# The first 40 microseconds of a fused graph-attention and gated-graph kernel: another route for adj's left halves, for the attention row and for the small weights, and other ranks

## The chip, the cores and the metric

The kernel runs on one core of one Trainium2 chip. The metric is the device time of one execution in microseconds. Three executions of the kernel before took 1454.94, 1455.84 and 1456.82 us; the median, 1455.84 us, is what the changed kernel is compared with. The profile is of one further execution.

A core has five engines, each with its own instruction stream executed in order: PE (TensorE, matrix products), DVE (VectorE), ACT (ScalarE), POOL (GpSimd) and SP (SyncE, here only an issuer of transfers). PE's loading of the stationary operand is listed as PEld. Transfers are issued on queues of SP, ACT and POOL and are carried by 16 DMA engines. Engines wait for each other by semaphores.

## The reference

There are 16 items x[b] of 1024 x 128, and one 0/1 matrix adj of 1024 x 1024, the same for all of them. Layer 0 is a graph attention:

```python
h = x @ others_weight
u1 = h @ a1;  u2 = h @ a2            # att_weight, two halves of 128
e = u1[:, idx1] + u2[:, idx2]        # pairs of neighbouring nodes
e = jnp.where(e >= 0, e, ALPHA * e)
att = jax.nn.softmax(jnp.where(adj > 0, e, NEG_BIG), axis=1)
x = layernorm(x + einsum('bik,bkl->bil', att, h) + x @ self_weight)
```

Layer 1 is five steps of a gated graph network, with h = x to begin with, and a second residual and normalisation at the end:

```python
m = adj @ h
u3 = h @ u3_w.T + u3_b
z = sigmoid([m, m] @ w3_w.T + w3_b + u3)
r = sigmoid([m, m] @ w4_w.T + w4_b + u3)
hv = tanh([m, m] @ w5_w.T + w5_b + (r * h @ u5_w.T + u5_b))
h = (1 - z) * h + z * hv
# after five steps: x = layernorm(x + h)
```

## The kernel before, in words

**Layout.** Of a matrix with 1024 rows, `NC` = 8 blocks of 128 rows lie on the 128 partitions; [...]nearly every matrix product is issued in halves of 512 columns. `adj` stays in SBUF for the whole run, in the type float32r; being 0 and 1 it is exact there. A product of a float32 matrix h with adj is made as two float32r products: `split` writes h's high part on ACT (`blk_h`, L636) and the remainder on DVE (L640), and `product` (L648) multiplies both with the same block of adj. Both parts together are the reference's float32 product. Other matrices (gates, h = x @ W) are multiplied in float32, which in the profile appear as two records for one instruction.

**Attention without a 1024 x 1024 softmax.** As e of one row depends on pairs of nodes, exponentials are taken once per column and not per entry. `wv_` (L414 to L423, DVE) forms the products of `others_w` with the two halves of the attention row; `spread_` (L767, PE) makes the scores of all nodes from item 0 on all partitions (`ps_p`); `lrelu_`, `exps_`, `exp_` and `larger_` (L770 to L783) turn them into `pb`, the exponentials. `z_` (L855, DVE, eight instructions of 128 x 512) multiplies each left half of adj with them and sums the rows. `rz_` (L874 to L878) takes the reciprocals, in two groups of four blocks for item 0. `hi_` and `lo_` (L907 ACT, L913 DVE) scale h by these into `blk`, and `po_` (L648 on `ps_acc_po`) multiplies `blk` with adj. The residual and self term is `px` (L970, L984), made with `wsi` = self_weight + identity. For items 4 to 7 that term is made ahead of time (L472, `ps_ahead`) and stored (PX). Item 1's exponentials are spread by L799. All other items have theirs fetched from DRAM.

**Gated steps.** Items go in pairs. For every pair and step, `ps_acc` collects adj times both items' h; `m`, `ps_g_r`, `gz` and `ps_g_v` are the gates' inputs, made with u3 (L1234), wm (L1244, L1260) and u5h (L1261). `wm`, `u5h` and the biases are prepared by `sums` after `own_weights`: one transposition on PE (L410, `ps_g_b`) turns the five bias rows into columns.

**Order.** Nothing is scheduled by the compiler. Every operation is put into a `Plan` with an engine, an estimated length, a rank, and the names it reads and writes. `Plan.order()` walks a model of time: whenever an engine is free it takes, of the operations whose inputs are there, the one with the lowest rank. The instructions are then issued in this order, and the hardware's engines follow it in order. Ranks come from the table `D` (one number per kind of operation) and from `NUDGE` (one number per item or per item and step). `dve`, `act`, `pe` and `sp` are one-line calls of `plan.add`; `lands` tells the plan when a transfer is thought to have landed.

**The start.** `early_loads` issues the first transfers on SP's and ACT's queues: x of item 0 in two halves, `others_w`, the attention row broadcast from DRAM to 128 partitions (128 KB, L351), adj as eight pieces of two row blocks by one half (512 KB each) into float32 tiles `staged[k][e]` (the trace calls them `blk_boot`), self_weight, x of item 1. `adj_tables(c)` casts these into `adj` (L494 for the left half, four on DVE and four on ACT; L497 for the right half, on ACT, which counts its row's ones as well). `late_loads` then sends ten small weights and biases (L381 to L388) from POOL's queue, after a copy that waits for the last piece of adj. `constants` writes the identity and some constants with POOL. Two fill matmuls (L440) and `IDLE` = 60 pairs of transposes of the identity (L436, rank 9000: taken when nothing else is ready in the plan) occupy PE; nobody reads their results. [...]

Of the kernel before, what the change touches and what calls it, by code (L numbers as in the profile page):

```python
# [10 lines left out]
F32 = mybir.dt.float32  # L11
F32R = mybir.dt.float32r
I32 = mybir.dt.int32
AF = mybir.ActivationFunctionType
# [3 lines left out]
P = 128  # L18
N = 1024
HALF = 512  # L20
NC = N // P
# [4 lines left out]
SHIFT = 40.0  # L26
# [6 lines left out]
AHEAD = range(4, 8)  # L33
LATE = 3001
TURNED = {(0, 0), (0, 1), (7, 2), (7, 3)}
IDLE = 60
NUDGE = {(3, 2): -0.6, (3, 3): 0.3, (0, 1): -0.5, (1, 1): 0.45, (2, 3): -0.2, (3, 1): -1.2, (3, 0): 0.6, (0, 2): 0.25, (2, 2): -0.6, (1, 4): -1.2, (1, 3): 0.3, (0, 3): -0.6, (1, 2): -0.15, (4, 0): -0.1, (2, 0): 1.2, (2, 1): 0.05, (4, 4): -0.3, (2, 4): -0.15, (7, 3): -0.75, (5, 4): 1.2, (4, 3): 1.25, (6, 3): -1.5, (6, 4): -0.6, (8, 2): 0.15, 10: 0.05, (11, 3): -1.2, (11, 4): 0.3, (7, 2): 0.3, (8, 3): -0.6, (12, 3): -0.45, (13, 3): -0.9, (12, 0): 1.15, (10, 3): -0.35, (8, 4): 0.05, (12, 4): -0.3, (12, 1): -0.05, (11, 2): -0.15, 12: -0.05, (13, 4): 1.2, (13, 0): 1.2, (11, 1): 0.05, (12, 2): 0.15, (10, 4): 0.1, (15, 0): -0.6, (14, 2): -0.6}


class Plan:  # L40
# [103 lines left out]
def kernel(  # L144
# [79 lines left out]
    def exact(pools):  # L224
# [48 lines left out]
        def T(t, dtype=None, shape=None):  # L273
            if t not in tiles:
                _, sh, dt, _ = kinds[t[0]]
                tiles[t] = places[t[0]].tile(
                    shape or sh, dtype or dt, tag=t[0], name="_".join(map(str, t)).replace("-", "n")
                )
            return tiles[t]
# [16 lines left out]
        def pe(*a, **k):  # L296
            plan.add("PE", *a, **k)

        def dve(*a, **k):
            plan.add("DVE", *a, **k)  # L300

        def act(*a, **k):
            plan.add("ACT", *a, **k)

        def sp(*a, **k):
            plan.add("SP", *a, **k)


        D = dict(m=-0.05, pu=1.4, u=0.95, pr=0.55, pz=0.85, r=0.25, pv=1.05, z=1.3, hv=-0.7, h=1.2, tr=2.55, o=6.35, ln=2.5, out=4.4, l1=-9, l2=-4, l3=-2, l4=-5.5, l5=-7.25)
        D.update(l6=-1.35, l7=-1, l8=-2, q=10, s=4.2, even=1, base=-1, q1=-6, b1=4, lz=-4, l1_0=-9, l2_0=-4, lz_0=-4, l3_0=-2, l4_0=-4, l5_0=-7, l6_0=-1.5, l7_0=-1, l8_0=-2)  # L310
        D.update(l1_1=-10, l2_1=-9, lz_1=-4, l3_1=-2, l4_1=-4, l5_1=-7, l6_1=-1.5, l7_1=-1, l8_1=-2, tab=8, tabc=1, cl=-5.9, ca=-50, cr=-51, px=-3.5, own=-2, ownw=-4.6)

        def on_pe(b, what):

# [20 lines left out]
        def W(name):  # L335
            return T(boot)[:, cols[name]]

        ws = ("T", "ws")
        staged = [[("blk", "boot", k, e) for e in range(2)] for k in range(NC // 2)]
        x0 = ("xt", 0)  # L340

        def adj_half(k, e):
            hs = slice(e * HALF, (e + 1) * HALF)
            rows = adj_t[2 * k * P : 2 * (k + 1) * P, hs].rearrange("(c p) n -> p c n", p=P)
            return T(staged[k][e], F32, [P, 2, HALF]), rows

        def early_loads():
            nc.sync.dma_start(T(x0)[:, HALF:N], x_t[0][:, HALF:N])
            nc.scalar.dma_start(T(x0)[:, 0:HALF], x_t[0][:, 0:HALF])
            nc.sync.dma_start(wo[:, 0:P], others_w)  # L350
            nc.scalar.dma_start(T(ws)[:, P : 3 * P], att_w.rearrange("k o -> o k").to_broadcast([P, 2 * P]))  # L351
            nc.sync.dma_start(*adj_half(0, 0))
            nc.scalar.dma_start(*adj_half(1, 0))
            nc.sync.dma_start(*adj_half(0, 1))
            nc.scalar.dma_start(*adj_half(1, 1))
            nc.sync.dma_start(W("ws"), self_w)
            for k in range(2, NC // 2):
                for e in range(2):
                    nc.sync.dma_start(*adj_half(k, e))
            nc.sync.dma_start(T(("xt", 1)), x_t[1])  # L360

        sp(
            9500,
            -103,
            early_loads,
            writes=[(boot, "early"), (ws, "early"), (x0, "early"), (("xt", 1), "early"), *((t, "early") for k in staged for t in k)],
        )

        def lands(ns, what):
            plan.add("DMA", ns, -103, lambda: None, writes=what, lag=0)  # L370

        lands(4700, [(x0, 0), (x0, 1)])
        lands(400, [(("wo",), 0), (ws, "att")])
        for ns, k, e in ((3600, 0, 0), (1400, 1, 0), (1000, 0, 1), (1400, 1, 1), (1600, 2, 0), (1400, 2, 1), (1400, 3, 0), (1400, 3, 1)):
            lands(ns, [(staged[k][e], 0), *([(boot, "ws")] if (k, e) == (2, 0) else [])])
        lands(1400, [(("xt", 1), 0), (("xt", 1), 1)])

        def late_loads():
            nc.gpsimd.tensor_copy(mark, T(staged[3][1])[0:1, 0, 0:1])
            for j, w in enumerate((w3_t, w4_t, w5_t)):  # L380
                nc.gpsimd.dma_start(  # L381
                    W("w345")[:, 256 * j : 256 * (j + 1)].rearrange("p (t e) -> p t e", t=2),
                    w.rearrange("(t p) e -> p t e", p=P),
                )
            nc.gpsimd.dma_start(u3, u3_t)
            nc.gpsimd.dma_start(u5, u5_t)
            for j, v in enumerate((w3_b, w4_b, w5_b, u3_b, u5_b)):
                nc.gpsimd.dma_start(T(ws)[j : j + 1, 3 * P : 4 * P], v.rearrange("(o p) -> o p", o=1))  # L388

        plan.add(  # L390
            "POOL",
            11000,
            -80,
            late_loads,
            reads=[(staged[3][1], 0)],
            writes=[(boot, "late"), (("uw",), 0), (ws, "b")],
            lag=2500,
        )

        def constants():  # L400
            make_identity(nc, ident)
            nc.gpsimd.memset(shift, -SHIFT)
            nc.gpsimd.memset(ones, 1.0)
            nc.gpsimd.memset(mhalf, -0.5)

        plan.add("POOL", 1400, -100, constants, writes=[(("ident",), 0), (("ones",), 0)])


        def column_(t, cols, n):
            nc.tensor.transpose(T(t)[:, 0:n], T(ws)[0:n, cols], ident[0:n, 0:n])  # L410

        def wv_():
            for two in range(2):
                nc.vector.scalar_tensor_tensor(  # L414
                    T(("look", "wv"))[:, two * P : (two + 1) * P],
                    wo[:, 0:P],
                    1.0,
                    T(ws)[:, (1 + two) * P : (2 + two) * P],
                    ALU.mult,
                    ALU.mult,  # L420
                    accum_out=wv[:, two : two + 1],
                )
            nc.vector.tensor_tensor(  # L423
                T(ws)[:, 0:P], wv[:, 0:1].to_broadcast([P, P]), wv[:, 1:2].to_broadcast([P, P]), ALU.add
            )
# [2 lines left out]
            nc.vector.tensor_copy(wo[:, P : P + 2], wv)  # L428
            nc.vector.tensor_copy(wo[:, P + 2 : P + 3], T(ws)[:, 0:1])

        dve(650, -101, wv_, reads=[(ws, "att"), (("wo",), 0)], writes=[(ws, 0), (("look", "wv"), 0)])
        dve(190, -65, wo_, reads=[(ws, 0)], writes=[(("wo",), 1)])

        def idle_():
# [55 lines left out]
        def adj_tables(c):  # L490
            st = staged[c // 2]

            def left(copy):
                copy(adj[:, c, 0:HALF], T(st[0])[:, c % 2])  # L494

            def right():
                nc.scalar.activation(adj[:, c, HALF:N], T(st[1])[:, c % 2], AF.Identity, accum_out=cnt[:, c : c + 1])  # L497

            if c < 4:
                dve(420, D["cl"], lambda: left(nc.vector.tensor_copy), reads=[(st[0], 0)], writes=[(("A",), c, 0)])  # L500
            else:
                act(A, D["ca"], lambda: left(nc.scalar.copy), reads=[(st[0], 0)], writes=[(("A",), c, 0)])
            act(640, D["cr"], right, reads=[(st[1], 0)], writes=[(("A",), c, 1)])

        def quarter(i, j):
            return lambda c: adj[:, 4 * i + c, j * HALF : (j + 1) * HALF]
# [149 lines left out]
        def layer0(b):  # L658
# [190 lines left out]
            rank = rank0(b) + lv("lz")  # L849
            for c in range(NC):  # L850

                st = staged[c // 2][0]

                def z_(c=c, st=st):
                    nc.vector.scalar_tensor_tensor(  # L855
                        T(junk),
                        T(st)[:, c % 2] if b == 0 else adj[:, c, 0:HALF].bitcast(F32),
                        1.0,
                        pairs()[:, c // 4, :],
                        ALU.mult,  # L860
                        ALU.mult,
                        accum_out=T(zs)[:, c : c + 1],
                    )

                entries = (st, 0) if b == 0 else (("A",), c, 0)
                dve(740, rank, z_, reads=[(pb, 0), (pb, 1), entries], writes=[(zs, c), (junk, 0)])


# [874 lines left out]
```

## Time and profile before

| what | us |
| --- | --- |
| median of three executions | 1455.84 |
| the profiled execution | 1455.08 |
| its span, first to last instruction | 1453.5 |
| PE busy | 1435.8 (99%) |
| DVE busy | 1159.7 (80%) |
| ACT busy | 897.4 (62%) |
| POOL busy | 193.5 (13%) |
| mean granted clock of PE | 0.997 |

Some landmarks of the first 60 us, from the order of time in the trace:

| event | us from the span's start |
| --- | --- |
| x of item 0 landed | 4.64 |
| attention row landed on all partitions | 7.06 |
| first piece of adj landed, last piece | 9.75, 18.11 |
| function table loaded on ACT | 10.89 to 12.17 |
| first and last row sum z of item 0 | 14.43, 22.37 |
| ten small loads issued by POOL | 18.30 to 25.89 |
| first product `ps_acc_po` of item 0 | 30.23 |
| transposition of the biases | 40.93 |
| first product `ps_acc` of the gated steps | 47.38 |

How to read it: a line of the order of time has the start, the duration (from the first start to the last end where several instructions stand in one line), the engine, the line of the kernel, the operation and "result <- inputs". A bracket at its end tells how long the engine was idle before it and what ended that. In tables by stage, each engine has its busy time in the stretch and the number of its instructions; then come PE's granted clock, the share of DMA engines busy, and the GB/s moved. An engine is busy also with work that nobody uses, such as the idle transposes.

### The profile page before, as it was taken

How to read it: one execution, taken by the hardware profiler on the slowest of the kernel's cores; microseconds unless marked ns; L12 is line 12 of the kernel's file. 1: busy time of each engine (PE TensorE's matmuls, PEld its weight loads, DVE VectorE, ACT ScalarE, POOL GpSimd, SP SyncE). 2: the span in 40 equal slices, each digit the busy share in tenths (PEclk: the TensorE clock that was granted, in tenths of full speed). 3: DMA queues.
4: the chain of work that ended last, by engine and by line, in shares of the span. 5: the costliest groups of instructions: out<-in, count | busy, mean ns of one | idle time of the engine just before them, and what ended most of it. 6: DMA issues, size and time to landing. Idle time of an engine off the chain costs nothing. (4 is left out here: it accounts for less than half of the span.)

```text
span 1453.5 us, 17779 instructions
## 1 busy us (share of the span) xinstructions
PE 1435.8 (99%) x5017; PEld 899.7 (62%) x5017; DVE 1159.7 (80%) x2752; ACT 897.4 (62%) x1793; POOL 193.5 (13%) x334
## 2 busy tenths in 40 slices
PE   9999999999999999999999999999999999999995
PEld 7666666566666666666656566666665666566562
DVE  5886989879889798888889698887988876865635
ACT  5665556656656766576656666566574766653644
POOL 1231001102010120111101121010210112000302
PEclk9999999999999999999999999999999999999998
DMA  7244235544344643354445543355423554223111
GB/s 283 95 125 152 60 109 160 162 136 126 82 133 131 181 132 102 100 176 131 116 116 145 152 124 81 103 172 162 120 75 94 153 161 113 74 66 87 36 37 32
DMA packets 187299, 174.28 MB, mean 120 GB/s; under 512 B 34408, under 2 KB 136504, under 8 KB 187192
## 3 DMA queue, kind: packets, MB, share of 16 engines
q1 hardware_dynamic: 180920, 155.23, 37.7%
q0 software_dynamic: 5168, 16.26, 3.4%
q10 hardware_dynamic: 1104, 1.57, 0.3%
q8 instruction: 41, 0.67, 0.2%
q14 instruction: 66, 0.54, 0.1%
HBM read 95.74 MB, written 77.24 MB: 119 GB/s over the span
## 5 line engine op out<-in xcount | busy, mean ns | idle before, releaser
L1261 PE MATMUL ps_g_v<-r,u5h 128*128 128x512 f32 x320 | 163.5, 592 | 0.0
L1260 PE MATMUL ps_g_v<-m,wm 128*128 128x512 f32 x320 | 163.4, 592 | 0.0
L1254 DVE SCALAR_TENSOR_TENSOR r<-r,hT 128x512 f32<-128x512 f32 x160 | 108.9, 685 | 64.1 <-ACT r L1247 63.4
L1244 PE MATMUL ps_g_r<-m,wm 128*128 128x512 f32 x320 | 159.0, 593 | 0.1
L1244 PE MATMUL gz<-m,wm 128*128 128x512 f32 x320 | 158.2, 592 | 0.0
L1269 DVE TENSOR_TENSOR hv<-hv,hT 128x512 f32<-128x512 f32 x160 | 109.7, 686 | 54.7 <-ACT hv L1266 53.7
L1234 PE MATMUL ps_g_r<-hT,u 128*128 128x512 f32 x320 | 152.7, 592 | 0.0
L1247 ACT ACTIVATE r<-ps_g_r,bh 128x512 f32<-128x512 f32 x160 | 109.4, 686 | 64.9 <-PE ps_g_r L1244 64.2
L648 PE MATMUL ps_acc_a<-tab,blk_s 128*128 128x512 f32 x544 | 147.8, 413 | 0.0
L648 PE MATMUL ps_acc_po<-adj,blk 128*128 128x512 f32 x512 | 139.6, 418 | 0.1
L1237 ACT COPY gz<-ps_g_r 128x512 f32<-128x512 f32 x160 | 91.3, 572 | 63.7 <-PE ps_g_r L1234 62.2
L648 PEld LDWEIGHTS ps_acc_a<-tab,blk_s 128*128 128x128 f32 x544 | 101.1, 188 | 33.3 <-issue 7.9
L1247 ACT ACTIVATE z<-gz,bh 128x512 f32<-128x512 f32 x160 | 109.6, 688 | 18.3 <-PE gz L1244 17.7
L648 PEld LDWEIGHTS ps_acc_po<-adj,blk 128*128 128x128 f32 x512 | 95.8, 188 | 35.1 <-issue 11.8
L1275 DVE SCALAR_TENSOR_TENSOR hT<-hv,hT 128x512 f32<-128x512 f32 x160 | 108.3, 679 | 1.5
L1272 DVE SCALAR_TENSOR_TENSOR hv<-z,hv 128x512 f32<-128x512 f32 x160 | 108.1, 677 | 0.6
L1261 PEld LDWEIGHTS ps_g_v<-r,u5h 128*128 128x128 f32 x320 | 60.5, 190 | 76.9 <-issue 62.0
L1244 PEld LDWEIGHTS gz<-m,wm 128*128 128x128 f32 x320 | 60.3, 189 | 74.8 <-issue 74.3
L606 DVE STREAM_TRANSPOSE T<-hT 128x512 f32<-128x512 f32 x138 | 95.4, 699 | 3.5 <-issue 1.8
L648 PE MATMUL ps_acc<-adj,blk_h 128*128 128x512 f32 x384 | 95.4, 402 | 1.0 <-ACT blk_h L636 0.8
L1260 PEld LDWEIGHTS ps_g_v<-m,wm 128*128 128x128 f32 x320 | 60.0, 190 | 57.6 <-issue 51.7
L640 DVE TENSOR_TENSOR blk_s<-G,blk_s 128x512 fp32r<-128x512 f32 x136 | 91.7, 680 | 3.0 <-ACT blk_s L636 2.7
(199 smaller groups left out, 2522.1 us busy)
## 6 DMA issues: line engine op xcount, KB each, us to landing
G<-X SPq DMA_DIRECT2D x140, 256.0 KB, 2.9
X<-T SPq DMA_DIRECT2D x552, 64.0 KB, 1.8
yd<-y POOLq DMA_DIRECT2D x32, 256.0 KB, 3.1
D_y<-T_y SPq DMA_DIRECT2D x112, 64.0 KB, 1.9
F_y<-D_y SPq DMA_DIRECT2D x28, 256.0 KB, 2.7
X<-y SPq DMA_DIRECT2D x28, 256.0 KB, 2.1
D_b<-T_b SPq DMA_DIRECT2D x112, 64.0 KB, 2.6
F_b<-D_b SPq DMA_DIRECT2D x28, 256.0 KB, 2.7
```

The costliest lines, as they stand in the source:

```text
L606: nc.vector.transpose(T(t).rearrange("p (b c i) -> p b c i", b=4, c=4), turned(src()))
L640: lambda: nc.vector.tensor_tensor(half(1), src(), half(0), ALU.subtract),
L648: nc.tensor.matmul(T(bank), T(blk)[:, k, c, :], right(c), start=(first and i == 0), stop=(last and i == len(terms) - 1), skip_group_check= ...
L1234: nc.tensor.matmul(T(pr), u3, h(), start=True, stop=True)
L1244: nc.tensor.matmul(T(p_), wm[:, j, :], T(m), start=False, stop=True, skip_group_check=True)
L1247: nc.scalar.activation(T(t), T(p_), AF.Tanh, bias=bh[:, j : j + 1], scale=0.5 * sg)
L1254: lambda r=r, h=h: nc.vector.scalar_tensor_tensor(T(r), T(r), 1.0, h(), ALU.add, ALU.mult),
L1260: nc.tensor.matmul(T(pv), wm[:, 2, :], T(m), start=True, stop=False)
L1261: nc.tensor.matmul(T(pv), u5h, T(r), start=False, stop=True)
L1269: nc.vector.tensor_tensor(T(hv), T(hv), h(), ALU.subtract)
L1272: nc.vector.scalar_tensor_tensor(T(hv), T(z), 1.0, T(hv), ALU.add, ALU.mult)
L1275: nc.vector.scalar_tensor_tensor(h(), T(hv), 0.5, h(), ALU.mult, ALU.add)
```

## The change

- The left halves of adj are no longer loaded into float32 tiles and cast by DVE and ACT. Four transfers of 512 KB on POOL's queue, issued right after the identity, read float32 from DRAM and write float32r into `adj`. The row sums z of item 0 read `adj` itself. The right halves come as before, all four on SP's queue now.
- The attention row is loaded to one partition (1 KB). A matmul with a row of ones (`pw_`, a new tile `ps_g_w` in the matrix accumulator) puts it on all partitions, and `wv_` reads it there.
- The ten small loads move from POOL's queue to SP's, behind the loads of items 2 and 3; the waiting copy on POOL is gone.
- `first_` runs one exponential of a single element on ACT, before anything else of ACT's but its two transfer issues; ones and shift are set before the identity.
- IDLE goes from 60 to 48 pairs.
- D and NUDGE have new numbers, so that from some 20 us on to the end of the kernel the instructions of all engines stand in another order. The last step of the last pair (items 14 and 15) is among what is rearranged: two u-products of item 14 come before the last accumulation of item 15, and the v-products of item 15's two halves stand together.

```diff
-IDLE = 60
-NUDGE = {(3, 2): -0.6, (3, 3): 0.3, (0, 1): -0.5, ...}
+IDLE = 48
+NUDGE = {(3, 2): -0.6, (3, 3): 0.75, (0, 1): -0.45, ...}
...
-        D = dict(m=-0.05, pu=1.4, u=0.95, pr=0.55, pz=0.85, r=0.25, ..., hv=-0.7, h=1.2, tr=2.55, ..., l2=-4, ...)
+        D = dict(m=-0.05, pu=1.4, u=0.95, pr=0.75, pz=0.85, r=0.45, ..., hv=0.5, h=1.2, tr=2.35, ..., l2=-7, ...)
...
-        staged = [[("blk", "boot", k, e) for e in range(2)] for k in range(NC // 2)]
+        staged = [("blk", "boot", k) for k in range(NC // 2)]
...
             nc.scalar.dma_start(T(x0)[:, 0:HALF], x_t[0][:, 0:HALF])
+            nc.scalar.dma_start(T(ws)[0:1, P : 3 * P], att_w.rearrange("k o -> o k"))
             nc.sync.dma_start(wo[:, 0:P], others_w)
-            nc.scalar.dma_start(T(ws)[:, P : 3 * P], att_w.rearrange("k o -> o k").to_broadcast([P, 2 * P]))
-            nc.sync.dma_start(*adj_half(0, 0))
-            nc.scalar.dma_start(*adj_half(1, 0))
-            nc.sync.dma_start(*adj_half(0, 1))
-            nc.scalar.dma_start(*adj_half(1, 1))
-            nc.sync.dma_start(W("ws"), self_w)
-            for k in range(2, NC // 2):
-                for e in range(2):
-                    nc.sync.dma_start(*adj_half(k, e))
+            for k in range(NC // 2):
+                nc.sync.dma_start(*adj_half(k))
+                if k == 1:
+                    nc.sync.dma_start(W("ws"), self_w)
...
         def late_loads():
-            nc.gpsimd.tensor_copy(mark, T(staged[3][1])[0:1, 0, 0:1])
             for j, w in enumerate((w3_t, w4_t, w5_t)):
-                nc.gpsimd.dma_start(
+                nc.sync.dma_start(
...
+        sp(5000, -80, late_loads, writes=[(boot, "late"), (("uw",), 0), (ws, "b")], lag=6000)
...
         def constants():
+            nc.gpsimd.memset(ones, 1.0)
+            nc.gpsimd.memset(shift, -SHIFT)
             make_identity(nc, ident)
...
+        def entries_():
+            for k in range(NC // 2):
+                nc.gpsimd.dma_start(adj[:, 2 * k : 2 * k + 2, 0:HALF], adj_rows(k, 0))
             nc.gpsimd.memset(mhalf, -0.5)
...
+        def first_():
+            nc.scalar.activation(mark, shift[0:1, :], AF.Exp)
+
+        act(1600, -104, first_, reads=[], writes=[(("mark",), 0)])
...
+        def pw_():
+            nc.tensor.matmul(T(pw)[:, 0 : 2 * P], ones[0:1, 0:1].to_broadcast([1, P]), T(ws)[0:1, P : 3 * P], start=True, stop=True)
...
-                    T(ws)[:, (1 + two) * P : (2 + two) * P],
+                    T(pw)[:, two * P : (two + 1) * P],
...
-            def left(copy):
-                copy(adj[:, c, 0:HALF], T(st[0])[:, c % 2])
-
...
-            if c < 4:
-                dve(420, D["cl"], lambda: left(nc.vector.tensor_copy), reads=[(st[0], 0)], writes=[(("A",), c, 0)])
-            else:
-                act(A, D["ca"], lambda: left(nc.scalar.copy), reads=[(st[0], 0)], writes=[(("A",), c, 0)])
...
-                        T(st)[:, c % 2] if b == 0 else adj[:, c, 0:HALF].bitcast(F32),
+                        adj[:, c, 0:HALF].bitcast(F32),
...
-                entries = (st, 0) if b == 0 else (("A",), c, 0)
+                entries = (("A",), c, 0)
```

## The prediction

> **What bounds the kernel now.** I read the page's busy row, the table by stage, the chain of waits on TensorE, and then the order of time at both ends.
>
> ```profile
> PE 1435.8 (99%) x5017; PEld 899.7 (62%) x5017; DVE 1159.7 (80%) x2752; ACT 897.4 (62%) x1793; POOL 193.5 (13%) x334
> ```
>
> TensorE (PE) is the bound, so a busy microsecond is worth something only if PE then has less to do, or waits less. The table by stage (span; busy time of PE, its weight loads, DVE, ACT, POOL; clock; DMA share; GB/s) shows where waiting is left:
>
> ```profile
> 0.00:10.00 10.00, 8.65 (x37) 5.97 (x38) 1.01 (x8) 0.00 (x0) 0.81 (x9) 1.00 0.68 226
> 10.00:20.00 10.00, 10.00 (x80) 8.36 (x79) 8.35 (x27) 9.10 (x24) 1.83 (x4) 1.00 1.05 387
> 40.00:60.00 20.00, 18.75 (x74) 12.35 (x73) 17.22 (x67) 14.66 (x39) 6.86 (x10) 1.00 0.37 119
> 60.00:80.00 20.00, 20.00 (x85) 13.68 (x84) 17.90 (x65) 12.48 (x33) 2.57 (x6) 1.00 0.25 72
> 1440.00:1454.00 14.00, 0.63 (x4) 0.42 (x4) 5.21 (x21) 3.29 (x8) 4.89 (x9) 0.62 0.28 82
> ```
>
> PE has 1.25 us of holes from 40 to 60 us, none from 60 to 80, and is done near 1443 us. But the first 40 us are full only in name. The same table for the idle transposes alone (L436: the identity against itself, nobody reads it):
>
> ```profile
> 0.00:10.00 10.00, 4.16 (x30) 4.15 (x30) 1.00 0.68 226
> 10.00:20.00 10.00, 5.74 (x50) 5.51 (x51) 1.00 1.05 387
> 20.00:30.00 10.00, 4.74 (x40) 4.27 (x40) 1.00 1.00 352
> ```
>
> 14.6 us of the first 30 are filler. PE executes in order, so filler ahead of real work is a delay whenever that work's inputs are ready. Are they? In the order of time:
>
> ```profile
> 7.09 0.29 DVE L414 SCALAR_TENSOR_TENSOR look_wv<-wo,T_ws 128x128 f32<-128x128 f32 x1 [7.09 <-DMA T_ws<-in_L_gnn_att_weight_dram]
> 8.92 1.88 PE L767 MATMUL ps_p<-xt,T_ws 128*128 128x512 f32 x4
> 10.89 1.28 ACT L779 ACT_TABLE_LOAD   x1 [10.89 <-PE ps_p L767]
> 11.32 0.76 DVE L494 CAST adj<-blk_boot 128x512 fp32r<-128x512 f32 x2
> 14.43 0.69 DVE L855 SCALAR_TENSOR_TENSOR junk<-blk_boot,pb 128x512 f32<-128x512 f32 x1
> 30.23 2.11 PE L648 MATMUL ps_acc_po<-adj,blk 128*128 128x512 f32 x8
> 47.38 0.49 PE L648 MATMUL ps_acc<-adj,blk_h 128*128 128x512 f32 x1 [0.76 <-ACT blk_h L636]
> ```
>
> The first real chain is attention row, column wv, spread p, exponentials, eight row sums z (L855, DVE), reciprocal, blk, po (L648). z ends at 22.4 and the last reciprocals at 23.3, yet po starts at 30.23: PE is simply behind, and every filler taken out ahead of po pulls everything after it forward. At 47.38 the first product of the next phase waits for ACT: there the chain, not PE, is late.
>
> **The change, part by part.**
>
> *Fillers, 120 to 96 transposes.* The two-record groups last 0.218 us, so 0.109 each once warm: 24 x 0.109 = 2.62. Against it stands one new matmul, the row spread by ones (128x256). A 128x512 of this kind takes two records of 0.429; half is 0.43. Net -2.19 on PE, all of it ahead of or inside the region where PE was never waiting.
>
> *Does PE then wait?* I walk the new order. The two fills end at 4.93 as before. 16 transposes follow; in the old trace they take 0.213 each until 6.3 us, then 0.109: six and ten make 2.4, so PE reaches the new matmul at 7.4. Its 1 KB row comes from a queue where the two halves of x have landed by 4.64: no wait. It ends at 7.8; DVE needs 0.85 for wv and its column (7.09 to 7.92 before), ready at 8.9. Ten transposes (1.09) bring PE to 8.9. So ps_p starts at 9.0, as before (8.92): the smaller load by itself gains nothing; I charge 0.1. From there 1.72 for ps_p, 1.79 for h, 34 transposes, pairs, 8, two px matmuls 1.72, 20, h of item 1 1.79, 4: the first po at 23.5. Before, 30.23. But 3.9 us of other work (two ahead matmuls 1.72, pairs 0.31, spread of item 1 1.9) has only changed sides, so the true lead is 2.8, or 2.4 after the four transposes (0.44) now standing behind po: the net of the fillers, within 0.2.
>
> *Is po fed by 23.5?* Exponentials: the function table is loaded right after ACT's DMA issues, so the 1.28 leaves the chain and the first runs near 11.0 instead of 12.19. DVE no longer casts four left halves (4 x 0.42 = 1.68), so larger and the first z come at 12.95 instead of 14.43 and the first reciprocals at 19.9 (before 21.0, in spite of a different interleaving), the second at 22.3. ACT loses four casts of 0.62. First blk halves: about 20.7. Slack to PE 2.8 us. So these edits cost and gain nothing directly; without them the PE lead would starve po by about 0-1 us.
>
> *Left halves by POOL's queue.* Now eight DVE row sums wait for casting transfers of 512 KB. Rows of before for that queue:
>
> ```profile
> yd<-y POOLq DMA_DIRECT2D x32, 256.0 KB, 3.1
> hT_boot<-in_L_gnn_w_w_dram POOLq DMA_DIRECT2D x3, 128.0 KB, 5.9
> ```
>
> The first is unloaded, the second in the stretch where the DMA engines are full (387 GB/s). POOL needs 0.8 per issue (2.40 for three), so four are out by 5. If this queue gets half of 390 GB/s, its 2 MB from 3.5 take 10.8: the last at 14.5 to 16. The pessimistic bound: the weights' 0.53 MB moved from 22.5 to 29.9, 71 GB/s, which would be 33 us. Those packets were short and few against long ones; here both queues carry rows of 2 KB, so I take 15.5. Row sums need left 2 at 17.6 and left 3 at 20.0; with PE's slack left 3 may come at 24.
>
> Two rules of the Trainium skill bear on this. The row first: DVE's first instruction is at 7.09 and it is busy 1.01 of the first 10 us. "SBUF — State Buffer", the box on the "DVE blocks DMA" trap, says that descriptors for GpSimd's transfers cannot be written while DVE runs a copy in a two-port mode, and advises a hardware queue. That speaks against the edit: held off behind four copies of 0.42 it would delay a transfer 1.7, which the 4 us of slack absorb; by the row, 0, since the issues end before DVE starts and those copies are gone. I take 0. "DMA: Bandwidth & Descriptors", Issuing engines are not separate DMA queues, says that a second issuer buys no bandwidth. The 387 GB/s row agrees that the engines were full; so I count no gain for loading, where a private path would bring 2 MB of adj 5 us sooner (2 MB at 390 GB/s). The sum is the same by both, as z is bound by DVE.
>
> *Ten small loads on SP.* POOL loses ten issues (18.3 to 25.9). SP gains ten, each 0.35 and paced by older landings; behind them wait one x, one piece ahead, and the PX stores. I estimate the last issue at 25.3, landing at 27.5 by an unloaded 2 us, 31 by the loaded 5.9; the nearest is the loaded end of a draining queue, 28. TensorE's transpose of the biases (L410), which blocks everything behind it, comes at 30.9 (40.93 before). Slack 3; bounds 0 and 0.3.
>
> *The stall at 47.* Holes from 46 to 52 in PE's starts: 0.92, 0.49 before the first products, 0.36 and three of 0.24 at the second b transposes, some small ones, 2.8 in all. In the new order the second b transposes stand behind more products, so that 1.1 should vanish; the first product still waits about 1.2. I book -1.5 (bounds -2.8 and +0.5).
>
> *Ranks anew.* Everything from 20 us on is reordered with the same work. Between 60 and 1420 PE had about 3 us of crumbs; closest distances: r to v 2.57 before, 3.43 after; transposed h to its product 3.74 before, 2.15 after, at two places, against about 2 us for ACT and DVE to split it. 0, bounds -2 and +2.
>
> *The end.* PE waits 0.8 and 3.64 for hT in the last 20 us. In the new last step two u-matmuls (1.72) stand earlier and the v of both halves together. Walked from the last accumulation's end to the last addition: 28.5 before, 26.2 + 1.72 after. I book -0.6 (bounds -1.2, +0.4).
>
> *Sum.* -2.2 + 0.1 - 1.5 - 0.6 = -4.2. The span of 1453.5 becomes 1449.3, and the profiled execution's 1455.08 (1.6 around the span) 1450.9. The median shown is 0.76 above that execution, so I state 1451.6 on its scale, -0.29%. Own range 1449.6 to 1452.9.
>
> **Rivals.**
> 1. *Only the fillers count.* The lead is given back at the first product after 46 us, because y, the normalisation and the splits are paced by DVE and POOL there (DVE is busy 17.22 of 20) and not by PE. For it: the wait at 47.38 is on ACT. Against: DVE also leads by 3.5 there, having lost 1.68 of casts. Then -2.2 or less: 1453.6, within the noise.
> 2. *The reordered middle gains too*: two of the three crumbs and the larger end, 1448.5. For it: longer r to v. Against: nearly no idle PE to win.
> 3. *Slower: the left halves are late.* Place: the fourth and third pair of row sums. With the 71 GB/s of the weights' row, left 3 lands at 33, po of the second group starves 9 us: -4.2 + 9 = +4.8, 1460.6. It costs from 24 us on (under 100 GB/s), eats the gain at 28.2 (85 GB/s). Against: equal packet lengths.
>
> **How the numbers follow.** A measurement tells about 0.2% (2.9 us) from nothing. Likeliest 0.50 and rival 2 0.12 are faster, 0.62; rival 1 0.23 is the same; rival 3 0.15. The range leaves out the outer half of rivals 2 and most of 3: 1448.7 to 1458.0.
>
> **What will show it.** Right: 96 transposes, 14.6 us of filler down to about 12; ps_p at 9.0; table load near 1.5; first z near 13; last left half before 20; the first accumulation's hole 1.2 or less; po of item 1 starting 3.6 earlier. Wrong: any L855 waiting on a DMA, L410 waiting for a load, or new holes over 1 us between 60 and 1420.

## The result, and the profile after

The changed kernel takes 1451.48 us (median of seven executions, 1449.74 to 1452.82); the kernel before, seven executions beside it, 1455.46 us (1454.94 to 1457.11). The ratio is 0.9971, with a 95% interval of 0.9959 to 0.9982. 1451.6 had been forecast. The profiled execution is the fastest of the seven: 1449.74 us, span 1447.6 us. That is 1.74 below its median, so the pair of traces shows a larger gain (5.34) than the medians (3.98).

The page's busy row and the table by stage of the changed kernel, with the columns of before:

```profile
PE 1432.1 (99%) x4995; PEld 898.2 (62%) x4995; DVE 1161.1 (80%) x2748; ACT 895.3 (62%) x1790; POOL 196.9 (14%) x327
```

```profile
0.00:10.00 10.00, 8.58 (x35) 5.23 (x36) 1.18 (x8) 1.49 (x2) 3.98 (x13) 1.00 0.85 280
10.00:20.00 10.00, 10.00 (x81) 8.54 (x80) 8.41 (x30) 8.94 (x27) 0.00 (x0) 1.00 1.10 392
40.00:60.00 20.00, 19.50 (x86) 14.21 (x85) 17.74 (x63) 13.98 (x39) 4.08 (x9) 1.00 0.29 93
60.00:80.00 20.00, 20.00 (x82) 12.93 (x81) 16.53 (x61) 12.96 (x36) 7.95 (x9) 1.00 0.27 81
```

PE is still the bound. From 40 to 60 us it is busy 19.50 us of 20, where it was 18.75. The idle transposes alone (L441):

```profile
0.00:10.00 10.00, 3.36 (x26) 3.11 (x26) 1.00 0.85 280
10.00:20.00 10.00, 5.92 (x51) 5.69 (x52) 1.00 1.10 392
20.00:30.00 10.00, 2.59 (x21) 2.12 (x19) 1.00 0.79 262
```

They sum to 11.9 us, from 14.6 (15.0 with the last two before, which ran after 30 us). The order of time, with the events that answer to those shown of before:

```profile
1.76 1.28 ACT L403 ACT_TABLE_LOAD   x1 [1.76 <-issue]
6.97 0.69 PE L414 MATMUL ps_g_w<-T_ws,ones 1*128 1x256 f32 x2
7.59 1.31 PE L441 MATMUL ps_idle<-ident 128*128 128x128 f32 x10
7.70 0.29 DVE L418 SCALAR_TENSOR_TENSOR look_wv<-wo,ps_g_w 128x128 f32<-128x128 f32 x1 [7.70 <-PE ps_g_w L414]
8.74 1.88 PE L763 MATMUL ps_p<-xt,T_ws 128*128 128x512 f32 x4
12.74 0.69 DVE L849 SCALAR_TENSOR_TENSOR junk<-adj,pb 128x512 f32<-128x512 f32 x1
23.38 0.70 PE L644 MATMUL ps_acc_po<-adj,blk 128*128 128x512 f32 x2
30.90 0.22 PE L409 MATMUL ps_g_b<-ident,T_ws 5*128 5x5 f32 x1
44.72 4.26 PE L644 MATMUL ps_acc<-adj,blk_h 128*128 128x512 f32 x16 [0.46 <-DVE us L730]
52.98 3.89 PE L644 MATMUL ps_acc_po<-adj,blk 128*128 128x512 f32 x16
```

The attention row is on all partitions 0.6 us later than by the broadcast (DVE starts at 7.70, before 7.09), yet ps_p starts no later (8.74, before 8.92), since transposes fill the way to it. First row sum 12.74 for 14.43, first po 23.38 for 30.23, bias columns 30.90 for 40.93, first product of the gated steps 44.72 for 47.38. Item 1's first product is at 52.98; before it stood at 57.01. The whole list of PE's waits, over the full span, now reads

```profile
PE ps_t L594 <- DVE hT L1269: 2.8, 2, 1.5
PE gz_fill L445 <- POOL ident masks.py:199: 1.4, 1, 1.4
PE ps_acc L644 <- DVE us L730: 0.5, 1, 0.5
PE ps_g_ph L686 <- DVE blk_h L636: 0.2, 1, 0.2
```

(us in total, times, longest). No wait on a transfer is among them. The wait for hT at the end was 4.4 in the same list of before.

Where the time went, in the two profiled executions, by three landmarks: to item 1's first product 57.01 became 52.98, -4.03; from there to the end of the last normalisation (L571 before, L567 after) 1390.66 became 1389.76, -0.90; from there to the end of the execution, with the last stores, 7.41 became 7.00, -0.41. I do not count the last piece as the change's: it is 7.14 and 6.78 where the code of before runs with fewer idle transposes.

The -4.03 can be split by the distance of PE's starts, as the same products stand ahead of item 1 in both kernels: transposes -3.14, the new matmul +0.62, the stall at 47 us -1.65, a later start of the fills +0.07, all else +0.1. Of the -3.14, only 2.62 are the 24 transposes. The rest is chance: the first transposes of an execution take 0.213 us each, the later ones 0.109, and here two were slow in the profile after and seven in the profile before. So some 0.5 of the -4.03 would be there between two executions of one kernel. Without it and the last piece, the traces give -4.4, and the medians say -3.98.

### The profile page after: what moved, and what is told of

It is laid out like the page before. It is cut to its first block, busy times and chain, and to the rows that moved or that the text cites. A ratio compares the mean times of both kernels' runs of the same rounds, so it can differ in the third digit from the quotient of the medians.

```text
span 1447.6 us, 17700 instructions
## 1 busy us (share of the span) xinstructions
PE 1432.1 (99%) x4995; PEld 898.2 (62%) x4995; DVE 1161.1 (80%) x2748; ACT 895.3 (62%) x1790; POOL 196.9 (14%) x327
## 4 chain that ended last, share of the span: by engine, by line
PE 95%; DVE 2%; POOL 1%; DMA 0%; ACT 0%; issue 0%; SPq 0%; POOLq 0%; DVEq 0%; ACTq 0%
PE ps_acc_a L644 17%; PE ps_g_r L1238 9%; PE gz L1238 9%; PE ps_g_v L1254 9%; PE ps_g_v L1255 9%; PE ps_g_r L1228 9%; PE ps_acc_c L644 9%; PE ps_acc_po L644 7%; PE ps_acc L644 6%; PE gz L644 4%; PE ps_g_ph L686 2%; PE ps_idle L441 1%; PE ps_acc_po L978 1%; PE ps_t L594 1%; PE ps_acc_px L964 1%; PE ps_ahead L477 0%
## 5 line engine op out<-in xcount | busy, mean ns | idle before, releaser
L644 PE MATMUL ps_acc_po<-adj,blk 128*128 128x512 f32 x512 | 143.7, 425 | 0.0
L644 PE MATMUL ps_acc<-adj,blk_h 128*128 128x512 f32 x384 | 100.8, 413 | 0.5 <-DVE us L730 0.5
```

The lines of the kernel that those rows point to most:

```text
L644: nc.tensor.matmul(T(bank), T(blk)[:, k, c, :], right(c), start=(first and i == 0), stop=(last and i == len(terms) - 1), skip_group_check= ...
```

## The experiments

All times are medians beside runs of the kernel before on the same chip (1455.5 us for the first four kernels, 1455.1 for the next four, 1455.02 for the last four). As these differ by 0.5, two other kernels are compared by their distances from the kernel before that ran beside each (-3.98 for the changed kernel). No kernel leaves out any part of the reference's computation; only transposes that nobody reads come or go.

### Fillers alone, ranks alone, with the plan made anew

Four kernels in which one part of the source was changed, the number of pairs or the ranks. The plan then computes the order again from the start to the end.

The kernel before with 48 pairs:

```diff
-IDLE = 60
+IDLE = 48
```

> The kernel before with 48 pairs of idle transposes for 60; nothing else. My theory (PE is simply behind until 40 us, so filler is delay): the first po at 27.6 instead of 30.23, the first ps_acc of the gated steps near 45 instead of 47.38, and 1.5 to 2.6 us off the time, 1453.3 on the scale of 1455.5. The rival (the lead is given back at the first ps_acc, because DVE, ACT and POOL pace it): po at 27.6 all the same, but ps_acc within 0.7 of 47.38 behind a longer wait, and 0 to 0.7 us off.

Measured: 1453.09 us, ratio 0.9985 (0.9978 to 0.9992), 2.4 us off. In the trace:

```profile
27.28 3.97 PE L648 MATMUL ps_acc_po<-adj,blk 128*128 128x512 f32 x16
44.44 0.49 PE L648 MATMUL ps_acc<-adj,blk_h 128*128 128x512 f32 x1 [0.76 <-ACT blk_h L636]
54.08 3.90 PE L648 MATMUL ps_acc_po<-adj,blk 128*128 128x512 f32 x16
```

Item 1 is at 54.08 for 57.01, and the lead is not given back at ps_acc: the wait is 0.76 in this kernel and in the kernel before (0.92 by the distance of PE's starts). But it is given back later, which neither theory has. Product by product against the kernel before, PE's lead is 2.96 near 600 us and 0.57 near 680, and the last normalisation ends only 0.46 earlier. Two of the new waits in its list, both between 655 and 659 us:

```profile
PE ps_g_r L1244 <- DVE m L1196: 0.7, 1, 0.7
PE gz L648 <- ACT blk_x L636: 0.3, 1, 0.3
```

This execution took 1454.35 us, more than the median. Of the 21 executions twelve took 1452.06 to 1453.30 and nine 1453.88 to 1454.68; whether the faster ones keep the lead is not known, as the profile is of one alone.

The changed kernel with 60 pairs:

```diff
-IDLE = 48
+IDLE = 60
```

> The changed kernel with its 60 pairs of idle transposes back; all else as changed. My theory: 2.6 us of PE's lead are gone, so the time is 2 to 2.6 us above the changed kernel's, near 1453.8, and the item 1 products that start at 52.98 in the changed kernel start near 55.5. The rival (the other edits of the start carry the gain, fillers only fill): within 0.7 of the changed kernel.

Measured: 1467.91 us, ratio 1.0087 (1.0074 to 1.0101): 16 us above the changed kernel. Neither theory held for the time. The new plan put all twelve extra pairs behind the first po, ten of them between 44 and 47 us, ahead of ps_acc and partly in its hole. Item 1 starts at 53.17 for 52.98, but with 24 products of ps_acc ahead of it in place of 32; the other eight, 2.0 us, stand behind. At equal work the start is thus some 2.2 later, 0.4 of it already lost at the spread of the attention row (7.39 for 6.97). The rest of the loss is spread over the middle. The longest of PE's waits, in a profile of the slowest of the five executions (1473.78 us; the others took 1467.69 to 1468.32):

```profile
PE ps_g_r L1238 <- ACT gz L1231: 8.5, 7, 3.4
PE ps_t L594 <- DVE hT L1269: 3.1, 3, 1.5
PE ps_acc_a L644 <- ACT m L1180: 2.0, 1, 2.0
```

Seven waits for ACT sum to 8.5 us, the longest of them 3.4 us near 316 us. Neither the kernel before nor the changed one has any of them. Twelve pairs of transposes at 20 us changed who stands before whom for 1400 us.

The kernel before with the new ranks:

```diff
-NUDGE = {(3, 2): -0.6, (3, 3): 0.3, ...}
+NUDGE = {(3, 2): -0.6, (3, 3): 0.75, ...}
...
-        D = dict(m=-0.05, pu=1.4, u=0.95, pr=0.55, ...)
+        D = dict(m=-0.05, pu=1.4, u=0.95, pr=0.75, ...)
```

> The kernel before with the new D and NUDGE, everything else as before. My theory: the ranks bring the end's 0.6 and perhaps the 1.1 at the second b transposes, so 0.5 to 1.7 us off the time (1454.4 on the scale of 1455.5); the start up to 30 us stays as it was. The rival (the ranks are the change, the start is only what they were made for): 3 to 4 us off. Third possibility: ranks fitted to the other start open new holes here and cost up to 2.

Measured: 1466.99 us, ratio 1.0084 (1.0070 to 1.0097), 11.5 us slower. Theory and rival missed; it is the third possibility, at several times its size.

The changed kernel with the old ranks (the same lines the other way round):

> The changed kernel with the old D and NUDGE. My theory: fillers and start stay, so 2.2 to 3.6 us below the kernel before, about 1452.5; the end is as before (28.5 us from the last accumulation to the last addition). The rival (ranks are the change): no difference from the kernel before, within 0.7.

Measured: 1461.87 us, ratio 1.0045 (1.0031 to 1.0058), 6.4 us slower than the kernel before and 10.4 slower than the changed one; both the theory and the rival missed. Its longest waits, without that for the first fill:

```profile
PE ps_t L594 <- DVE hT L1269: 4.4, 2, 3.6
PE ps_acc L644 <- DVE blk_h L636: 1.5, 1, 1.5
PE ps_acc_po L644 <- DVE yT L928: 1.3, 1, 1.3
PE ps_g_v L1255 <- DVE r L1248: 1.0, 1, 1.0
PE ps_t_b L594 <- ACT y L561: 1.0, 1, 1.0
```

The old wait at the end is back (4.4), as expected. Not expected: in the table by stage PE is idle for 2.7 us from 40 to 60 and for 3.5 from 80 to 160, where it is idle for 0.5 and 0.2 in the changed kernel. What follows from the four: a set of ranks is worth something only with the start for which it was found. Each of the two crossings of start and ranks costs more than the whole change brings, and a comparison in which the plan is made anew does not measure the edit.

### Fillers alone, with the order kept

So the next kernels keep the plan's order on every engine and change only what an operation emits. For the idle transposes the pair's number is handed to the emitter (both variants in one cut):

```diff
-        def idle_():
-            for j in range(2):
+        def idle_(i):
+            for j in range(2) if i < 36 else ():    # 24 fewer; or, 24 more:
+            for j in 2 * list(range(2)) if 34 <= i < 46 else range(2):
```

> The changed kernel's order kept as it is on all engines, with 24 more idle transposes emitted at the places where the last 24 of the 48 pairs stand (20 become 40, 4 become 8). So only PE's filler differs. My theory: first po 2.6 later (26.0 for 23.38), item 1's products at 55.5 for 52.98, and 2.0 to 2.6 us more time than the changed kernel, 1453.8. The rival (fillers are hidden behind DVE and ACT): 0 to 0.7 more. The 16 us that the re-planned version with 60 pairs cost would then be the reordering's, with no hole over 1 us between 60 and 1420 here.

Measured: 1453.12 us, ratio 0.9985 (0.9978 to 0.9991), 2.0 us above the changed kernel. PE in the order of time:

```profile
26.57 0.71 PE L644 MATMUL ps_acc_po<-adj,blk 128*128 128x512 f32 x2
47.92 4.26 PE L644 MATMUL ps_acc<-adj,blk_h 128*128 128x512 f32 x16 [0.46 <-DVE us L730]
56.19 2.03 PE L644 MATMUL ps_acc_po<-adj,blk 128*128 128x512 f32 x8
```

Each is 3.2 us later than in the changed kernel: 2.62 for the 24 transposes, and 0.57 that this execution had already lost when it came to the spread of the attention row (7.54 for 6.97, see the last section). The wait ahead of ps_acc is 0.46, as it was. The last normalisation ends at 1445.86 for 1442.74, the same 3.1. There are no holes over 1 us in the middle, so most of the 16 us of the re-planned kernel were the reordering's. In the medians I had expected 2.0 to 2.6 and find 2.0.

> The changed kernel's order kept, with the last 24 idle transposes not emitted. PE could reach the first po at 20.8; its first operand was there at 21.1. My theory: 1.5 to 2.2 us below the changed kernel, 1449.6. The rival (in the changed kernel PE's lead is used up and the chain through DVE and ACT is the bound from here): first po near 21.3, but the wait before the first ps_acc grows from 0.6 to 2 us or more, and 0 to 0.5 us is gained.

Measured: 1447.69 us, ratio 0.9949 (0.9935 to 0.9962): 7.4 us below the kernel before and 3.4 below the changed one, more than expected. In the trace:

```profile
19.40 0.60 PE L441 MATMUL ps_idle<-ident 128*128 128x128 f32 x4
20.85 2.02 PE L686 MATMUL ps_g_ph<-wo,xt 128*128 128x131 f32 x16 [0.84 <-ACT blk L901]
22.62 1.64 PE L644 MATMUL ps_acc_po<-adj,blk 128*128 128x512 f32 x6
43.52 4.27 PE L644 MATMUL ps_acc<-adj,blk_h 128*128 128x512 f32 x16 [0.47 <-DVE us L730]
51.79 2.26 PE L644 MATMUL ps_acc_po<-adj,blk 128*128 128x512 f32 x9
```

Of the 2.62 removed, 1.0 comes back as a hole at 19.8 before item 1's h; the name in the bracket (ACT's blk) was done at 20.1, so what PE waited for is another thing: x of item 1. The trace counts the arrivals of that transfer, and the last of its 16 came at 20.71 (in the changed kernel at 17.75, long before PE was there). Item 1's products start 1.2 earlier. The trace places 1.2 us, or 1.5 if the 0.35 lost at the start of this execution is counted out; the medians differ by 3.4. The two intervals, 0.9935 to 0.9962 and 0.9959 to 0.9982, just overlap, so they do not show the larger value; 1.2 us would be 0.08%. The traces cannot decide it either: that of the changed kernel is of the fastest of seven executions, this one of the slowest of five.

The order of the kernel before, with its last 24 transposes not emitted (`i < 48`):

> The order of the kernel before kept on all engines, with its last 24 idle transposes not emitted: the fillers alone, without the re-planning of the run with 48 pairs. My theory: po at 27.6, ps_acc near 44.7, no new holes at 624 and 655, so 2.3 to 2.9 us below the kernel before, 1452.8. The rival (the old start feeds po no earlier): po later than 29, 0 to 1 us below.

Measured: 1452.87 us, ratio 0.9985 (0.9978 to 0.9991), 2.2 us off.

```profile
27.57 3.97 PE L648 MATMUL ps_acc_po<-adj,blk 128*128 128x512 f32 x16
44.74 0.49 PE L648 MATMUL ps_acc<-adj,blk_h 128*128 128x512 f32 x1 [0.76 <-ACT blk_h L636]
54.37 3.90 PE L648 MATMUL ps_acc_po<-adj,blk 128*128 128x512 f32 x16
```

The lead of 2.64 arrives whole at 54 us, with the same 0.76 of wait at ps_acc. But I had expected no hole near 655, and this execution has one of 1.5 us that ends at 658.4, in the list of waits:

```profile
PE ps_g_r L1244 <- DVE m L1196: 1.5, 1, 1.5
```

PE's lead falls there from 2.66 to 0.93, and the last normalisation ends 0.73 earlier than before. So in the old order most of the lead can be given back, 600 us later than the rival of the prediction had it, at a place where a result of DVE was not ready as much earlier as PE was. In the new order the two kernels above keep their distance from the changed one (3.2 behind at 60 us and 3.1 at 1400; 0.7 ahead at both). The medians of the two kernels in the old order (2.2 and 2.4 us off) suggest that not every execution loses as much as these two.

### The edits of the start, with the order kept

The left halves by the hardware queues again, with four casts on DVE and four on ACT, and no casting transfers:

```diff
-            for k in range(NC // 2):
-                nc.gpsimd.dma_start(adj[:, 2 * k : 2 * k + 2, 0:HALF], adj_rows(k, 0))
...
             def right():
+                if c >= 4:
+                    nc.scalar.copy(adj[:, c, 0:HALF], T(("blk", "left", c // 2))[:, c % 2])
...
                 def z_(c=c):
+                    if b == 0 and c < 4:
+                        nc.vector.tensor_copy(adj[:, c, 0:HALF], left)
```

> The changed kernel's order kept, with the left halves loaded to float32 tiles by the hardware queues as in the kernel before, four of them cast by DVE right before their row sums and four by ACT right before the right halves of the same rows; no casting transfers. My theory: DVE gets 1.7 us more and ACT 2.5 before the first blk; PE's slack of 2.5 us takes most of it, so 0 to 1.2 us more than the changed kernel. The rival (the casts off DVE and ACT are what made the gain): 2 us or more, with po waiting until 25 or later. Another (casting transfers cost something): up to 0.5 less.

Measured: 1451.62 us, ratio 0.9977 (0.9969 to 0.9985): 0.5 above the changed kernel, within the intervals.

```profile
12.70 0.42 DVE L856 CAST adj<-blk_left 128x512 fp32r<-128x512 f32 x1
21.01 1.00 ACT L909 ACTIVATE blk<-hx,rz 128x128 fp32r<-128x128 f32 x3
23.50 0.71 PE L649 MATMUL ps_acc_po<-adj,blk 128*128 128x512 f32 x2
```

The casts are there and the first blk is 1.6 us later (21.01; 19.43 in the changed kernel), but PE reaches po at 23.50. It had not been waiting, so nothing is lost there: of the 0.12 to 23.38, all had been lost at the spread of the attention row (7.10 for 6.97). What is lost comes at the very end. The last normalisation ends at 1442.55, 0.2 before the changed kernel's, but from there the execution takes 8.5 us more, and in the changed kernel 7.0. The last section says where.

Three edits undone together: left halves as above, no early exponential, and the attention row broadcast from DRAM without the matmul by ones. Beside the lines above:

```diff
         def first_():
-            nc.scalar.activation(mark, shift[0:1, :], AF.Exp)
+            pass
...
-            nc.scalar.dma_start(T(ws)[0:1, P : 3 * P], att_w.rearrange("k o -> o k"))
+            nc.scalar.dma_start(T(ws)[:, P : 3 * P], att_w.rearrange("k o -> o k").to_broadcast([P, 2 * P]))
...
         def pw_():
-            nc.tensor.matmul(T(pw)[:, 0 : 2 * P], ones[0:1, 0:1].to_broadcast([1, P]), ...)
+            T(pw)
```

> The changed kernel's order with its 48 pairs, and three edits of the start undone together: left halves loaded by hardware queues and cast, no early exponential, attention row broadcast from DRAM. Ranks, fillers and the small weights on SP stay as changed. My theory: with all three late together the first blk comes near 22.3 to 22.8 (19.4 in the changed kernel, 21.0 with the casts alone), so PE waits up to 0.5 us at po, and the time is 0 to 1.0 us above the changed kernel. The rival (the three carry the gain together though not singly): 2 us or more.

Measured: 1451.97 us, ratio 0.9979 (0.9970 to 0.9988), 0.9 above the changed kernel, inside the noise. PE starts po at

```profile
23.11 0.71 PE L649 MATMUL ps_acc_po<-adj,blk 128*128 128x512 f32 x2
```

even earlier than in the changed kernel, since the matmul by ones is gone. The first blk came at 21.46, not at 22.3 or later as expected, and there is no wait at po. The last normalisation ends 1.2 later than in the changed kernel, with new holes near 483 and 923 us (0.55 and 0.47), and the end takes 8.7 us for 7.0. So the 0.9 says little of the three edits themselves.

With 24 transposes fewer, the same edits undone one at a time:

> The changed kernel's order with 24 fewer idle transposes, and the left halves again loaded by hardware queues and cast by DVE and ACT. With 48 pairs the casts cost nothing, since PE came to po at 23.5 while blk was there near 22. With the fillers gone PE waits for blk: in the run with 48 pairs the first blk came 1.6 us later with the casts (21.0 for 19.4 on ACT). My theory: 0.8 to 2.0 us more than with casting transfers at the same fillers (1447.7 on the scale of 1455.1), so about 1449. The rival (the casts find room on DVE and ACT here too): within 0.5.

> The changed kernel's order with 24 fewer idle transposes, and without the early exponential, so that ACT loads its table when the first score is there. My theory: the exponentials and row sums come 1.2 us later, PE waits for it before po, 0.6 to 1.2 us more than the run with 24 fewer transposes. The rival (another wait is longer, so the table's is covered): within 0.4 of it.

> The changed kernel's order with 24 fewer idle transposes, and the attention row again broadcast from DRAM to all partitions, without the matmul by ones. PE has 0.5 us less to do, DVE reads the row when it lands (7.06 before) and ps_p starts after the 26 transposes near 8.3 instead of 8.8. My theory: up to 0.5 us less or no difference; the spread by TensorE gains nothing. The rival (the small load is what lets adj come in early): row sums wait for transfers, 0.5 to 2 us more.

| 24 fewer transposes, and | us | ratio | item 1's first product | last normalisation ends |
| --- | --- | --- | --- | --- |
| all edits in | 1447.69 | 0.9949 (0.9935 to 0.9962) | 51.79 | 1442.00 |
| left halves cast again | 1450.56 | 0.9967 (0.9955 to 0.9979) | 52.10 | 1442.23 |
| no early table load | 1449.37 | 0.9959 (0.9946 to 0.9973) | 51.96 | 1442.60 |
| row broadcast from DRAM | 1449.68 | 0.9961 (0.9948 to 0.9975) | 52.00 | 1442.71 |

All three medians are above that of the kernel with all edits, by 3.0, 1.8 and 2.1 us, each further than its theory or its rival had it. In the traces only 0.2 to 0.3 of it is at item 1, and 0.2 to 0.7 at the last normalisation. The 0.6 and 0.7 of the last two contain a wait of 0.5 and 0.7 near 921 us, which is no part of the start. And 1.7 of the 3.0 with the casts is the longer end again (8.57 us after the last normalisation, for 6.91). The trace names what holds PE ahead of po now (the casts first, then the broadcast):

```profile
21.15 2.02 PE L691 MATMUL ps_g_ph<-wo,xt 128*128 128x131 f32 x16 [1.04 <-DMA xt<-in_x_dram]
```

```profile
21.04 2.02 PE L686 MATMUL ps_g_ph<-wo,xt 128*128 128x131 f32 x16 [1.82 <-DMA xt<-in_x_dram]
```

x of item 1 is issued behind all of adj, and its last arrival is at 21.01 and 20.90. That landing covers the casts, and the broadcast row as well (ps_p there starts at 8.31 and 1.8 us of wait follow). Without the early exponential the last arrival was at 18.33 and PE did not wait for x; the first po starts at 21.38 and then waits for DVE's blk, three times, 1.0 us in all:

```profile
22.30 0.74 PE L644 MATMUL ps_acc_po<-adj,blk 128*128 128x512 f32 x2 [0.45 <-DVE blk L907]
23.44 0.96 PE L644 MATMUL ps_acc_po<-adj,blk 128*128 128x512 f32 x3 [0.41 <-DVE blk L907]
```

Even so item 1 is only 0.2 late. Whether the table load would show itself behind an x that lands near 21, these runs do not tell. Whether the rest of the differences in the medians is real stays open too: their intervals overlap, and I have no line of a trace for it. The weights moved to SP's queue were put back in no run.

## Why the prediction was right

*PE is simply behind, so filler is delay.* Right. 24 more transposes in the same order moved po, ps_acc and item 1 by 2.62 plus what that execution had lost before them; 24 fewer in the order of before brought 2.64 at 54 us. The new matmul was booked at 0.43 and takes 0.62 (6.97 to 7.59 above), so the term is -2.00 where -2.19 was booked. The medians give 2.0 for the 24 and 2.2 for those of before.

*The walk of the new start.* ps_p at 9.0, measured 8.74; first row sum 12.95, 12.74; po 23.5, 23.38; the bias transposition 30.9, 30.90. The first reciprocals ended at 19.5 (19.9). Two errors partly cancel at ps_p: six slow transposes were counted and two came, and the new matmul is longer than booked.

*"These edits cost and gain nothing directly."* Not contradicted: three of them undone cost 0.9, within the interval, and the longer end alone would account for it. The remark beside it, that without them po would starve by 0 to 1 us, was not borne out: in that kernel PE waits nowhere at po. The slack was booked at 2.8; DVE's first blk ends at 21.14 and po starts at 23.38, 2.2. The casts used 1.6 of it.

*The stall at 47.* -1.5 booked, -1.65 by PE's starts. (The table by stage has the holes from 40 to 60 at 1.25 and 0.50; it counts the modelled ends of the products as busy.) The 1.1 at the second b transposes vanished. The hole at the first product is 0.62 plus 0.27 in place of 0.92 plus 0.49; I had left it at 1.2. The gain goes with the order: with fewer fillers in the old order the holes are as before, and with the three edits undone in the new order they are as in the changed kernel. No run separates it from the small weights' new queue.

*Left halves by POOL's queue.* The trace gives these transfers

```profile
adj<-in_adj_dram POOLq DMA_DIRECT2D x4, 512.0 KB, 10.1
```

(median us to landing), and of the same line alone

```profile
DMA to landing us min/median/max: 7.8/10.1/13.7
```

The last is issued at 3.86 and landed at 17.5 us, where I took 15.5, and before the row sum at 19.44 that needs it. No row sum waits for it. POOL issued from 1.5 to 4.6, DVE started at 7.70: the trap that the Trainium skill tells of ("SBUF — State Buffer", the box on DVE blocking a software DMA) had no occasion here, and no run tried it with DVE busy. That a second issuer brings no bandwidth ("DMA: Bandwidth & Descriptors", Issuing engines are not separate DMA queues) agrees with 392 GB/s from 10 to 20 us after, 387 before. Where the engines were not full it did carry more: from 4 to 6 us 370 GB/s for 92, where in the kernel before SP issued nothing from 2.6 to 4.7 us. But no row sum had waited for a transfer before either.

*Small loads on SP.* The last one is issued by 26.0 (25.3 estimated), and nothing waits at 30.90.

*Ranks anew: 0, bounds -2 and +2.* The number holds, as a statement on this start with these ranks: between item 1 and the last steps the two traces differ by 0.3, and no hole over 1 us stands between 60 and 1420. What the prediction did not see is that the term hangs on the pairing; with the old ranks the same start loses 10.4 us, and in the old order the lead of the start was mostly lost near 657 us in both profiles. Had the ranks been fitted less well, no argument of mine from the closest distances in the order would have told. To that extent the number was luck.

*The end.* -0.6 booked. From the end of the last accumulation to the last normalisation 28.5 became 27.9, counting the two u-products that moved ahead of it, and PE's waits for hT went from 4.4 to 2.8. That is read from the traces; no run has the new last step alone.

*The rivals.* That the lead is given back at the first ps_acc is shown wrong: the wait there is the same with 24 fillers more or fewer in the new order and with 24 fewer in the old, so the chain that it waits for moves with PE: in the changed kernel the profile names DVE's us, which DVE reads from PE's transposition right ahead of that product. It can be given back later, as the two kernels in the old order show near 657 us. Late left halves did not occur. The larger gain (1448.5) lies 3 us below what was measured; PE's crumbs in the middle stayed as they were.

*The sum.* -4.2 booked, -3.98 measured, with an interval from -6.0 to -2.6. That 1451.6 and 1451.48 agree to 0.1 is luck; that the terms of the start, the stall and the end came out near their sizes in the traces is not.

## What to carry to other kernels

Filler on the bounding engine is work; look at the table by stage for the filler alone, and take it out as far as the next operand's arrival, which has to be found anew each time (here DVE's blk at 21.1 us, and x of item 1, which landed between 17.75 and 20.71 us in four kernels with the same transfers). Where an order is computed from ranks, test an edit with the order kept and only the emission changed, and find the ranks again afterwards: a new plan can move the time by more than any edit does. An edit that takes work off an engine with slack need not be worth anything by itself: here it was 0 at po for eight casts. And a lead that has arrived at one landmark is not yet a gain: follow it to the end of the kernel.

## What was not expected of the hardware

The first transposes run at half speed (0.213 us each, then 0.109), and how long they do differs between executions of the same instructions. Up to the spread of the attention row, PE executes two fills and 16 transposes in all kernels with the changed start that have this matmul; it comes to it at 6.97 in the changed kernel and, in two others, at

```profile
6.53 0.69 PE L414 MATMUL ps_g_w<-T_ws,ones 1*128 1x256 f32 x2
```

```profile
7.54 0.69 PE L414 MATMUL ps_g_w<-T_ws,ones 1*128 1x256 f32 x2
```

a spread of 1.0 us, while the granted clock in the table by stage reads 1.00 from the start. The Trainium skill ("TensorE: Matmul & The Clock Gate", Part 1) says that the window after which the clock opens runs freely and does not begin with the kernel; that would give such a spread. It is a good part of what limits a comparison of two profiled starts.

From the end of the last normalisation to the end of the span it takes 4.7 to 5.9 us in eleven kernels and 6.75 to 6.9 in the three that load left halves by hardware queues in the changed order (to the end of the execution 6.5 to 7.4, and 8.5 to 8.7). The kernel before loads them so too and takes 5.9. The stores are not it: the last one has landed 3.0 to 3.3 us after the normalisation in these three, 2.98 in the changed kernel. It is in the closing instructions, which the views leave out. The trace has a first DRAIN of ACT there, which the other engines wait for: it starts 0.07 us after ACT's instruction before it in eleven kernels, and 2.23 to 2.29 us after it in the three. Why ACT is late there stays open, but it comes after all results are in DRAM, and 1.5 to 1.7 us of the three profiled times are due to this longer end.
